# Local attention's q and k: projected by tokens and transposed, or projected by features

## The chip, the cores and the metric

The kernel runs on one core of a Trainium2 chip. The metric is device time in microseconds of one execution, as the median of several runs. Engines are named as in the profile: PE (TensorE, with PEld for its weight loads), DVE (VectorE), ACT (ScalarE), POOL (GpSimd) and SP (SyncE, whose queue issues all DMAs here).

## The reference

Eight sequences of 512 tokens with 128 features pass through a linear attention layer (16 heads, second-order Taylor features), a residual sum, and then six layers of local attention and a gated feed-forward network. The change is in the local attention, whose part of the reference is, for each layer:

```python
q, k, v = split(x @ Wqkv)                 # 16 heads of 64
q = l2norm(q) * qs;  k = l2norm(k) * ksc  # l2norm: t / max(|t|, 1e-12)
q = q * cos * scale + rotate_half(q) * sin * scale
k = k * cos * inv + rotate_half(k) * sin * inv      # inv = 1 / scale
# windows of 32 tokens; each sees itself and the window before
sim = einsum('bhwie,bhwje->bhwij', bq, bk2) * 8.0
attn = softmax(where(mask, -max, sim), -1)
out = einsum('bhwij,bhwje->bhwie', attn, bv2) @ Wo
# rotate_half([x1, x2]) = [-x2, x1], halves of 32
```

All of it is in float32.

## The kernel before

A first stage (some 500 us) computes the linear attention for all eight sequences. Then the six layers run over units: one unit is a block of 128 tokens of one sequence in one layer, 6 x 8 x 4 = 192 units in all. A loop over slots `t` starts one unit per slot; the steps of a unit are spread over several slots by `at(t, lag, step)`, which runs the step for unit `t - lag`. Each sequence's activations stay in SBUF, by features, in `state[b]` (128 features x 513 tokens). After the last of the four units of a sequence the feed-forward steps follow, in four successive slots: `feed_norm`, `feed_first` (transposes of the normalised tokens), `feed_middle` (three hidden chunks with Gelu, lines 667 to 675) and `feed_last` (w2, line 702).

PE's instructions run in the order in which the loop writes them (`manual_schedule`). The order on the other engines is made by the tile framework when it builds the program: it places instructions by their readiness in its own plan, puts those in `high_priority` ahead, and keeps what `issue_behind` asks for. Each engine then works through its list strictly in order.

Of PSUM's eight banks, four are two buffers of tag "mm" (projections, values, hidden chunks, w2), two are two buffers of tag "tr" (transposes), and two are the one buffer of tag "s". That last one is used in turn by `out_project` (py, line 642), `weigh_values` (po, line 613), and `masked` and `scores` (sp, lines 558 and 572). A step that takes a buffer waits until all readers of the one that had it before are done.

The steps of a unit before the change:

- `proj` (lag 0): q and k are projected with the tokens as the stationary operand, so that the result has tokens on partitions and 1024 columns (16 heads x 64) in PSUM. Line 451 is its matmul. DVE multiplies it by two tables out of PSUM (`turned`, line 459, and `straight`, line 467), ACT squares it (line 475, two halves), POOL sums the two products (line 482).
- `sum_squares`: DVE reduces the squares to one number for each token and head (line 485). `unit_length`: ACT takes the root of its inverse as Exp(-0.5 Ln) (lines 96 and 98), POOL bounds it (line 495) and multiplies q and k by it (line 498).
- `values`, `spread` (lag 0): v is projected (line 509), copied to SBUF by ACT (line 514) and spread over two windows' partitions by ten DMAs (lines 523 to 526).
- `by_features` (lag 1): 16 transposes by PE (line 70) and four copies by ACT (line 548) turn q and k to features on partitions: qT, kT. POOL copies the last 32 tokens of kT ahead for the next unit (line 551).
- `masked` (lag 1): ACT writes the mask into sp. `scores` (lag 1): 64 matmuls of 64x32 tiles add q k on top (line 572); DVE takes the maxima (line 580); ACT computes sixteen exps of 128x64 with the negated maximum as bias, one for each head (line 584); DVE sums the weights (line 590).
- `by_keys`, `weigh_values` (lag 2): transposes of the weights, copies pT by ACT (line 602), 64 matmuls with v (line 613), and the division by the sums on DVE (line 621).
- `out_by_features` (lag 2), `out_project` (lag 3): transposes, copies oT by ACT (line 635), eight matmuls with Wo (line 642) and the sum onto `state` by DVE (line 647).

Three `addr_align` calls pad PE's instruction stream at certain places.

The first stage has a root that goes through DRAM: `head_norm` sums squares by matmuls into 32 PSUM rows each (line 324), takes the root (lines 329 and 331), writes it to the DRAM tile `roots` (line 334) and reads it back spread over partitions (line 338); line 340 multiplies by it on DVE.

Of the kernel before, what the change touches and what calls it, by code (L numbers as in the profile page):

```python
# [15 lines left out]
P = 128  # L16
# [7 lines left out]
FILL = 16  # L24
IN_STEP = 98
# [3 lines left out]
def sandwich_kernel(ctx: ExitStack, tc: tile.TileContext, ins: dict, out: bass.AP):  # L29
# [23 lines left out]
    roots = [dram.tile([2, 2, 2, N], F32, tag=f"roots_{i}", name=f"roots_{i}") for i in range(2)]  # L53
    state = [const.tile([P, N + 1], F32, tag=f"state_{b}", name=f"state_{b}") for b in range(B)]
# [5 lines left out]
    vec = const.tile([P, NV + 1], F32, tag="vec", name="vec")  # L60
    g_c, b_c, b2_c = (vec[:, i * DEPTH : (i + 1) * DEPTH] for i in range(3))
    b1_c = vec[:, 3 * DEPTH : NV].rearrange("p (c l) -> p c l", l=DEPTH)
    gw = vec[:, NV : NV + 1]

# [8 lines left out]
    tables, exps, divisions, copies, pcopies, maxima = [], [], [], [], [], []  # L73
# [7 lines left out]
    def gelu_only():  # L81
        ld = nc.scalar.preload_act_table_set("gelu_and_others")
        issue_behind(ld, pcopies[-1])
        issue_behind(ld, exps[-1])
        tables.append(ld)
# [53 lines left out]
    HF = HD // 2  # L139
# [33 lines left out]
    for a in range(2):  # L173
        nc.vector.memset(of[HD * a : HD * (a + 1), a::2], 1.0)
    eps4 = const.tile([P, 1], F32, tag="eps4", name="eps4")
# [112 lines left out]
    def weigh(k):  # L288
# [14 lines left out]
        if s == len(STEPS) - 1:  # L303
# [3 lines left out]
                [P, 2, NB, P], F32, tag=("qT", "pT", "on", "oT", "sq", "sq")[i], name="yT"  # L307
# [92 lines left out]
    rot = const.tile([P, 4, NB, HD], F32, tag="rot", name="rot")  # L400
    nc.sync.dma_start(rot, ins["rotary"].rearrange("k (n p) d -> p k n d", p=P))
    qks = const.tile([P, 2, DEPTH, HD], F32, tag="qks", name="qks")
    for s, nm in enumerate(("q_scale", "k_scale")):
        nc.sync.dma_start(
            qks[:, s].rearrange("p l d -> p (l d)"),
            ins[f"L0_ffn_{nm}"].rearrange("l d -> (l d)").partition_broadcast(P),
        )

    def load_layer(l):
# [13 lines left out]
        tab = wl.tile([P, 4, NB, HD], F32, tag="tab", name=f"tab_{l}")  # L423
        for s in range(2):
            sc = qks[:, s, l, :]
            nc.gpsimd.tensor_tensor(
                tab[:, 2 * s], rot[:, 2 * s], sc.unsqueeze(1).to_broadcast([P, NB, HD]), ALU.mult
            )
            for a, o in ((0, HF), (HF, 0)):
                nc.gpsimd.tensor_tensor(  # L430
                    tab[:, 2 * s + 1, :, a : a + HF],
                    rot[:, 2 * s + 1, :, a : a + HF],
                    sc[:, o : o + HF].unsqueeze(1).to_broadcast([P, NB, HF]),
                    ALU.mult,
                )

        return dict(wqkv=wqkv, wo=wo, w1=w1, w2=w2, tab=tab)

    def proj(u, s):

        L, b, j = u["L"], u["b"], u["j"]
        wqkv, tab = L["wqkv"], L["tab"]
        lhs = state[b][:, j * P : (j + 1) * P]
        if s == 0:
            u["ss"] = f2.tile([P, 2, H], F32, tag="ss", name="ss")
            u["qk"] = f2.tile([P, 2, H, 2, HF], F32, tag="qk", name="qk")
        ss, qk = u["ss"], u["qk"]

        ps = psum.tile([P, 2, H, HF], F32, tag="mm", name="mm")
        for a in range(2):  # L450
            nc.tensor.matmul(  # L451
                ps[:, a].rearrange("p h d -> p (h d)"), lhs, wqkv[:, s, a, :], start=True, stop=True
            )
        sq = f2.tile([P, H, 2, HF], F32, tag="sq", name="sq")
        t1 = f2.tile([P, 2, H, HF], F32, tag="t1", name="t1")
        t2 = f2.tile([P, 2, H, HF], F32, tag="t2", name="t2")

        def turned():
            nc.vector.tensor_tensor(  # L459
                t2, ps[:, ::-1],  # L460
                tab[:, 2 * s + 1, j, :].rearrange("p (a d) -> p a d", a=2).unsqueeze(2)
                .to_broadcast([P, 2, H, HF]),
                ALU.mult,
            )

        def straight():
            nc.vector.tensor_tensor(  # L467
                t1, ps,
                tab[:, 2 * s, j, :].rearrange("p (a d) -> p a d", a=2).unsqueeze(2)
                .to_broadcast([P, 2, H, HF]),  # L470
                ALU.mult,
            )

        def squared(a):
            nc.scalar.activation(sq[:, :, a, :], ps[:, a], AF.Square)  # L475

        turned()
        straight()
        squared(0)
        squared(1)  # L480
        u["sq", s] = sq
        nc.gpsimd.tensor_tensor(qk[:, s].rearrange("p h a d -> p a h d"), t1, t2, ALU.add)  # L482

    def sum_squares(u, s):
        su = nc.vector.tensor_reduce(  # L485
            u["ss"][:, s], u["sq", s].rearrange("p h a d -> p h (a d)"), AX.X, ALU.add
        )
        if divisions:
            issue_behind(su, divisions[-1])

    def unit_length(u):

        ss, qk = u["ss"], u["qk"]
        inverse_root(ss, ss)
        nc.gpsimd.tensor_scalar(ss, ss, 1e12, None, ALU.min)  # L495
        for i in range(2):
            t = qk[:, i].rearrange("p h a d -> p h (a d)")
            nc.gpsimd.tensor_tensor(  # L498
                t, t, ss[:, i, :].unsqueeze(2).to_broadcast([P, H, HD]), ALU.mult
            )  # L500

# [10 lines left out]
    def spread(u):  # L512
        j, v0 = u["j"], u["v0"]
        cp = nc.scalar.copy(v0, u.pop("v0ps"))
        if copies:
            issue_behind(cp, copies[-1])
# [15 lines left out]
    def by_features(u, c, which=(0, 1)):  # L532

        j, qk, B_ = u["j"], u["qk"], u["B"]
        if c == 0:
            u["qT"] = f1.tile([P, NP, P], F32, tag="qT", name="qT")
            if j == 0:
                B_["kT"] = f2.tile([P, NP, W + P], F32, tag="kT", name="kT")
                nc.gpsimd.memset(B_["kT"][:, :, :W], 0.0)
            u["kT"] = B_["kT"]  # L540
        for s in which if isinstance(which, tuple) else (which,):
            ps = psum.tile([P, 4, P], F32, tag="tr", name="tr")
            for i in range(4):
                h0 = 2 * (c + i)
                transposed(ps[:, i, :], qk[:, s, h0 : h0 + 2].rearrange("p h a d -> p (h a d)"), P, P)
            dst = u["qT"][:, c : c + 4, :] if s == 0 else u["kT"][:, c : c + 4, W:]
            with tc.high_priority():
                copies.append(nc.scalar.copy(dst, ps))  # L548
        if c == NP - 4 and s == 1 and j < NB - 1:
            B_["kT"] = f2.tile([P, NP, W + P], F32, tag="kT", name="kT")  # L550
            nc.gpsimd.tensor_copy(B_["kT"][:, :, :W], u["kT"][:, :, P:])

    def masked(u):

        u["sp"] = sp = psum.tile([P, 2, NP, 2 * W], F32, tag="s", name="sp", bufs=1)
        mk = mask0 if u["j"] == 0 else mask
        with tc.high_priority():
            sd = nc.scalar.copy(
                sp.rearrange("t p c k -> t (p c) k"), mk.unsqueeze(1).to_broadcast([P, H, 2 * W])
            )  # L560
        issue_behind(sd, copies[-1])

    def scores(u):

        qT, kT = u["qT"], u["kT"]
# [13 lines left out]
        with tc.high_priority():  # L579
            maxima.append(nc.vector.tensor_reduce(mx, sp, AX.X, ALU.max, negate=True))  # L580
        pe = f2.tile([P, NP, 2, 2 * W], F32, tag="pe", name="pe")
        for pair in range(NP):
            for p in range(2):
                ex = nc.scalar.activation(  # L584
                    pe[:, pair, p, :], sp[:, p, pair, :], AF.Exp, bias=mx[:, p, pair : pair + 1]
                )
                issue_behind(ex, tables[-1])
        exps.append(ex)
        su = f2.tile([P, NP, 2], F32, tag="su", name="su")
        nc.vector.tensor_reduce(su, pe, AX.X, ALU.add)  # L590
        nc.vector.reciprocal(su, su)
        u["pe"], u["su"] = pe, su
# [69 lines left out]
    def feed_hidden(u, c):  # L662
# [5 lines left out]
        nc.tensor.addr_align(FILL, offset=FILL // 2)  # L668
        nc.tensor.matmul(pg[:cn, 1], w1[:, c0 : c0 + cn], xnT, start=True, stop=True)  # L669
        if c < NCH - 1:  # L670
            nc.tensor.addr_align(FILL, offset=FILL // 2)
# [85 lines left out]
    with tc.manual_schedule(engines={mybir.EngineType.PE}):  # L757
# [8 lines left out]
        for t in range(len(units) + 7):  # L766
# [7 lines left out]
            gelus = 0 <= t - 5 < len(units) and units[t - 5]["j"] == NB - 1  # L774
            at(t, 0, proj, 0)
            at(t, 0, proj, 1)


            if t % NB == 1 and NB < t < len(units):
                nc.tensor.addr_align(128, offset=IN_STEP)  # L780
            if t % NB == 3 and NB < t < len(units):
                nc.tensor.addr_align(FILL)
            at(t, 2, by_keys)
            if gelus:
                gelu_only()
            at(t, 3, out_project)
# [5 lines left out]
            at(t, 1, by_features, 0)  # L792
            at(t, 2, weigh_values)
            at(t, 1, by_features, 4, 0)
            at(t, 1, masked)
            at(t, 0, values)
            if t == 3:
                to_state(B - 1)
            at(t, 0, sum_squares, 0)
            at(t, 0, sum_squares, 1)  # L800
            if not gelus:
                at(t, 0, unit_length)
            at(t, 1, by_features, 4, 1)
            at(t, 0, spread)
            at(t, 3, feed_norm, ends=True)
            at(t, 4, feed_first, ends=True)

# [121 lines left out]
```

## Time and profile before

| what | value |
|---|---|
| median of 3 runs | 3645.83 us (3638.61 to 3646.25) |
| profiled execution, first to last instruction | 3641.2 us |
| granted PE clock, mean | 0.993 |
| PE matmuls busy | 3575.2 us (98%), 65184 instructions |
| PE weight loads busy | 2404.3 us (66%) |
| DVE busy | 2796.4 us (77%) |
| ACT busy | 2765.6 us (76%) |
| POOL busy | 1843.6 us (51%) |
| DMA queue, share of 16 engines | 25.2%, 240.93 MB |

Busy time counts an instruction from its start to its end, and matmuls overlap, so a PE that is 98% busy is not one at its peak. Idle time of an engine matters only where another waits for it. In the groups, a line counts two records for each float32 matmul and one for each transpose. The profile names each instruction by line, engine, operation and output <- input.

### The profile page before, as it was taken

Reading aid. Unit: us, or ns where it says so; the run is one execution under the profiler, and the core shown is the slowest. Engines: PE = TensorE matmul, PEld = TensorE weight load, DVE = VectorE, ACT = ScalarE, POOL = GpSimd, SP = SyncE. Lnnn points to the kernel's source line nnn. Section 1 sums busy time; section 2 is a strip of 40 time slices with the busy share of each in tenths; the row PEclk is TensorE's granted clock in tenths of the full one; section 3 lists DMA queues with packets and bytes.
Section 4 is the critical chain, followed back from the end, with each engine's and each line's share of the span. In section 5 each row is a group of like instructions: output and inputs, shape, how many; then the busy total and the mean of one; then the engine's idle time right before and its main releaser. Section 6 shows DMA issues by size and latency. Waiting matters only on the chain.

```text
span 3641.2 us, 153034 instructions
## 1 busy us (share of the span) xinstructions
PE 3575.2 (98%) x65184; PEld 2404.3 (66%) x65184; DVE 2796.4 (77%) x3915; ACT 2765.6 (76%) x6864; POOL 1843.6 (51%) x1311
## 2 busy tenths in 40 slices
PE   8999989999999999999999999999999999999997
PEld 4555556666766666676766766667676676766765
DVE  4555567887878788787887878878787887878885
ACT  4555557787888888888787888888878787887875
POOL 0000045555655556555565655556555565556652
PEclk9999999999999999999999999999999999999998
DMA  3121132222232222232222322223222222222221
GB/s 109 46 53 47 42 89 68 65 65 69 79 77 72 65 64 71 77 81 68 61 69 68 87 72 69 65 65 86 71 71 69 60 70 64 66 68 73 74 74 47
DMA packets 158598, 250.73 MB, mean 69 GB/s; under 512 B 33774, under 2 KB 54508, under 8 KB 157164
## 3 DMA queue, kind: packets, MB, share of 16 engines
q1 hardware_dynamic: 157932, 240.93, 25.2%
q8 instruction: 530, 8.68, 1.0%
q14 instruction: 136, 1.11, 0.1%
HBM read 41.31 MB, written 4.46 MB: 13 GB/s over the span
## 4 chain that ended last, share of the span: by engine, by line
PE 87%; ACT 9%; DVE 2%; issue 1%; DMA 1%; POOL 0%; SPq 0%; POOLq 0%; DVEq 0%; ACTq 0%
PE tr L70 19%; PE mm L451 14%; PE py L642 10%; PE mm L509 9%; PE po L613 8%; PE sp L572 6%; ACT pe L584 4%; PE mm L667 4%; PE mm L669 4%; PE y L299 3%; PE py L702 3%; PE sc L269 2%; PE po L348 2%; ACT L76 1%; PE vv L247 1%; ACT oT L635 1%
## 5 line engine op out<-in xcount | busy, mean ns | idle before, releaser
L482 POOL TENSOR_TENSOR qk<-t,t 128x1024 f32<-128x1024 f32 x384 | 910.9, 2372 | 619.1 <-DVE t L467 424.7
L498 POOL TENSOR_TENSOR qk<-qk,ss 128x1024 f32<-128x1024 f32 x384 | 722.4, 1902 | 16.0
L451 PE MATMUL mm<-wqkv,state 128*128 128x512 f32 x1536 | 700.3, 596 | 0.6 <-issue 0.6
L584 ACT ACTIVATE pe<-sp,mx 128x64 f32<-128x64 f32 x3072 | 652.0, 381 | 2.4 <-DVE mx L580 2.3
L459 DVE TENSOR_TENSOR t<-mm,tab 128x1024 f32<-128x1024 f32 x384 | 468.3, 1219 | 220.3 <-PE mm L451 214.9
L475 ACT ACTIVATE sq<-mm 128x512 f32<-128x512 f32 x768 | 420.6, 605 | 127.4 <-DVE t L467 120.9
L467 DVE TENSOR_TENSOR t<-mm,tab 128x1024 f32<-128x1024 f32 x384 | 468.1, 1219 | 5.9
L451 PEld LDWEIGHTS mm<-wqkv,state 128*128 128x128 f32 x1536 | 273.1, 190 | 289.8 <-issue 242.4
L485 DVE TENSOR_REDUCE ss<-sq 128x16 f32<-128x1024 f32 x384 | 448.4, 1209 | 0.1
L70 PE MATMUL tr<-ident,qk 128*128 128x128 f32 x3072 | 440.9, 276 | 1.8 <-ACT qT L548 0.8
L70 PEld LDWEIGHTS tr<-ident,qk 128*128 128x128 f32 x3072 | 351.3, 141 | 120.7 <-issue 56.3
L642 PE MATMUL py<-oT,wo 128*128 128x128 f32 x3072 | 379.3, 277 | 0.3 <-ACT oT L635 0.3
L642 PEld LDWEIGHTS py<-oT,wo 128*128 128x128 f32 x3072 | 368.1, 196 | 0.5 <-ACT oT L635 0.5
L509 PE MATMUL mm<-wqkv,state 128*128 128x512 f32 x768 | 362.9, 595 | 2.6 <-DVE t L467 2.6
L635 ACT COPY oT<-tr 128x512 f32<-128x512 f32 x384 | 205.5, 587 | 168.1 <-PE tr L70 165.5
L572 PEld LDWEIGHTS sp<-kT,qT 64*32 64x32 f32 x24576 | 264.2, 105 | 91.3 <-issue 54.3
L613 PE MATMUL po<-v,pT 64*32 64x64 f32 x24576 | 297.0, 225 | 9.6 <-issue 3.9
L548 ACT COPY qT<-tr 128x512 f32<-128x512 f32 x384 | 226.3, 589 | 99.6 <-PE tr L70 99.1
L613 PEld LDWEIGHTS po<-v,pT 64*32 64x32 f32 x24576 | 268.8, 105 | 46.0 <-PE tr L70 24.6
L572 PE MATMUL sp<-kT,qT 64*32 64x64 f32 x24576 | 297.6, 225 | 0.3 <-issue 0.3
L495 POOL TENSOR_SCALAR ss<-ss 128x32 f32<-128x32 f32 x192 | 54.7, 285 | 478.7 <-ACT ss L98 470.8
L548 ACT COPY kT<-tr 128x512 f32<-128x512 f32 x384 | 225.6, 588 | 74.8 <-PE tr L70 74.5
(110 smaller groups left out, 5243.9 us busy)
## 6 DMA issues: line engine op xcount, KB each, us to landing
v<-v SPq DMA_DIRECT2D x1152, 128.0 KB
v<-v SPq DMA_DIRECT2D x672, 64.0 KB
rs<-roots SPq DMA_DIRECT2D x64, 256.0 KB
wqkv<-in_L_ffn_Wqkv_dram SPq DMA_DIRECT2D x6, 1536.0 KB
wo<-in_L_ffn_Wo_dram SPq DMA_DIRECT2D x6, 512.0 KB
xin<-_attn_hidden_states_dram SPq DMA_DIRECT2D x8, 256.0 KB
xr<-_attn_hidden_states_dram SPq DMA_DIRECT2D x8, 256.0 KB
x<-xr SPq DMA_DIRECT2D x8, 256.0 KB
```

What stands on the lines that cost most here:

```text
L70: nc.tensor.transpose(ps[:cols, :rows], src, ident[:rows, :rows])
L451: nc.tensor.matmul(ps[:, a].rearrange("p h d -> p (h d)"), lhs, wqkv[:, s, a, :], start=True, stop=True)
L459: nc.vector.tensor_tensor(t2, ps[:, ::-1], tab[:, 2 * s + 1, j, :].rearrange("p (a d) -> p a d", a=2).unsqueeze(2) .to_broadcast([P, 2, H, ...
L467: nc.vector.tensor_tensor(t1, ps, tab[:, 2 * s, j, :].rearrange("p (a d) -> p a d", a=2).unsqueeze(2) .to_broadcast([P, 2, H, HF]), ALU.mult,)
L482: nc.gpsimd.tensor_tensor(qk[:, s].rearrange("p h a d -> p a h d"), t1, t2, ALU.add)
L498: nc.gpsimd.tensor_tensor(t, t, ss[:, i, :].unsqueeze(2).to_broadcast([P, H, HD]), ALU.mult)
L509: nc.tensor.matmul(ps[:, p, :], lhs, L["wqkv"][:, 2, p, :], start=True, stop=True)
L548: copies.append(nc.scalar.copy(dst, ps))
L572: nc.tensor.matmul(sp[W * w : W * (w + 1), p, pair, :], qT[HD * p : HD * (p + 1), pair, W * w : W * (w + 1)], kT[HD * p : HD * (p + 1), pa ...
L584: ex = nc.scalar.activation(pe[:, pair, p, :], sp[:, p, pair, :], AF.Exp, bias=mx[:, p, pair : pair + 1])
L613: nc.tensor.matmul(po[W * w : W * (w + 1), p, pair, :], pT[r, pair, W * w : W * (w + 1)], v2[r, w, HD * pair : HD * (pair + 1)], start=(pa ...
L642: nc.tensor.matmul(py, L["wo"][:, c, :], oT[:, c, :], start=(c == 0), stop=(c == NP - 1))
```

## The change

q and k are now projected with the weights as the stationary operand, 128 features (two heads) at a time, so that they come out with features on partitions, and the transposes and copies of `by_features` go. The halves of a head are no longer beside each other on one partition, so the order of features in the weights and tables is permuted in such a way that rotating by half is a swap of 16 with 16 partitions inside each group of 32: a DVE `stream_shuffle`. POOL takes over the product with the second table.

The squares' sums now run over partitions: 16 matmuls with a matrix of ones (`per_head`), each into 32 PSUM rows. The roots of k are written to a DRAM tile `lengths` and read back spread over 64 partitions each, and POOL multiplies k by them into kT. The roots of q are not multiplied into q: they are transposed by PE (`lengths_by_tokens`) to one number for each token and head, and are given to the exps as their scale; the negated maxima are multiplied by them first, on DVE.

The steps behind the scores have moved by one slot (`by_keys`, `weigh_values` lag 3, `out_project` lag 4, feed-forward steps each one later), `values` and `spread` run one slot later too, and the sum of the weights is a step of its own a slot after the exps. The tables are loaded from DRAM for each layer and scaled on POOL. The pads in PE's stream and several `issue_behind` go.

```diff
     def proj(u, s):
-        ps = psum.tile([P, 2, H, HF], F32, tag="mm", name="mm")
-        for a in range(2):
-            nc.tensor.matmul(
-                ps[:, a].rearrange("p h d -> p (h d)"), lhs, wqkv[:, s, a, :], start=True, stop=True
-            )
...
-        turned()
-        straight()
-        squared(0)
-        squared(1)
-        nc.gpsimd.tensor_tensor(qk[:, s].rearrange("p h a d -> p a h d"), t1, t2, ALU.add)
+        ps = psum.tile([P, NP, P], F32, tag="mm", name="mm")
+        for c in range(NP):
+            nc.tensor.matmul(
+                ps[:, c], L["wqkv"][:, s].rearrange("p a c -> p (a c)")[:, c * P : (c + 1) * P],
+                state[b][:, tok], start=True, stop=True,
+            )
...
+        with tc.high_priority():
+            nc.scalar.activation(sq, ps, AF.Square)
+        nc.vector.stream_shuffle(t2.rearrange("p c n -> p (c n)"), ps.rearrange("p c n -> p (c n)"), swap)
+        nc.vector.tensor_tensor(t1, ps, tab[0], ALU.mult)
+        nc.gpsimd.tensor_tensor(t2, t2, tab[1], ALU.mult)
+        nc.gpsimd.tensor_tensor(u["qk"][:, s], t1, t2, ALU.add)
...
-    def sum_squares(u, s):
-        su = nc.vector.tensor_reduce(
-            u["ss"][:, s], u["sq", s].rearrange("p h a d -> p h (a d)"), AX.X, ALU.add
-        )
+    def sum_squares(u):
+        u["ms"] = ms = psum.tile([P, 2, P], F32, tag="tr", name="ms")
+        for s in range(2):
+            sq = u.pop(("sq", s))
+            for r in range(2):
+                for i in range(4):
+                    nc.tensor.matmul(
+                        ms[W * i : W * (i + 1), s], per_head[:, r], sq[:, 2 * i + r],
+                        start=(r == 0), stop=(r == 1), skip_group_check=True,
+                    )
...
     def unit_length(u):
-        inverse_root(ss, ss)
-        nc.gpsimd.tensor_scalar(ss, ss, 1e12, None, ALU.min)
-        for i in range(2):
-            t = qk[:, i].rearrange("p h a d -> p h (a d)")
-            nc.gpsimd.tensor_tensor(
-                t, t, ss[:, i, :].unsqueeze(2).to_broadcast([P, H, HD]), ALU.mult
-            )
+        rt = f2.tile([P, 2, P], F32, tag="rt", name="rt")
+        with tc.high_priority():
+            inverse_root(rt, u.pop("ms"))
+        nc.gpsimd.tensor_scalar(rt, rt, 1e12, None, ALU.min)
+        rd = lengths[u["j"] % 2]
+        for a in range(2):
+            nc.sync.dma_start(rd[a], rt[8 * a : P : 16, 1])
+        rs = f1.tile([P, NP, P], F32, tag="rs", name="rs")
+        for a in range(2):
+            nc.sync.dma_start(
+                rs[HD * a : HD * (a + 1)].rearrange("p c n -> p (c n)"),
+                rd[a].rearrange("c n -> (c n)").partition_broadcast(HD),
+            )
...
+        nc.gpsimd.tensor_tensor(u["kT"][:, :, W:], u["qk"][:, 1], rs, ALU.mult)
+        if u["j"] < NB - 1:
+            B_["kT"] = f2.tile([P, NP, W + P], F32, tag="kT", name="kT")
+            nc.gpsimd.tensor_copy(B_["kT"][:, :, :W], u["kT"][:, :, P:])
+
+    def lengths_by_tokens(u):
+        ps = psum.tile([P, H, 8], F32, tag="tr", name="qr")
+        transposed(ps.rearrange("p h k -> p (h k)"), u.pop("rt")[:, 0], P, P)
+        u["qr"] = qr = f2.tile([P, NP, 2], F32, tag="qr", name="qr")
+        nc.vector.tensor_copy(qr.rearrange("p c a -> p (c a)"), ps[:, :, 0])
...
-    def by_features(u, c, which=(0, 1)):
...
     def scores(u):
...
             maxima.append(nc.vector.tensor_reduce(mx, sp, AX.X, ALU.max, negate=True))
+            nc.vector.tensor_tensor(mx, mx, qr.rearrange("p c a -> p a c"), ALU.mult)
...
                 ex = nc.scalar.activation(
-                    pe[:, pair, p, :], sp[:, p, pair, :], AF.Exp, bias=mx[:, p, pair : pair + 1]
+                    pe[:, pair, p, :], sp[:, p, pair, :], AF.Exp,
+                    bias=mx[:, p, pair : pair + 1], scale=qr[:, pair, p : p + 1],
                 )
...
             at(t, 0, proj, 0)
             at(t, 0, proj, 1)
-            at(t, 2, by_keys)
+            at(t, 3, by_keys)
+            at(t, 0, sum_squares)
+            at(t, 0, unit_length)
...
-            at(t, 3, out_project)
+            at(t, 4, out_project)
...
-            at(t, 1, by_features, 0)
-            at(t, 2, weigh_values)
-            at(t, 1, by_features, 4, 0)
+            at(t, 3, weigh_values)
+            at(t, 2, weight_sums)
             at(t, 1, masked)
-            at(t, 0, values)
+            at(t, 1, values)
...
+            at(t, 0, lengths_by_tokens)
+            at(t, 7, feed_last, ends=True)
             at(t, 1, scores)
```

## The prediction

> **What bounds the kernel now.** The page's head first, then the chain that ended last, then the timeline of one steady slot, instruction by instruction.
>
> ```profile
> PE 3575.2 (98%) x65184; PEld 2404.3 (66%) x65184; DVE 2796.4 (77%) x3915; ACT 2765.6 (76%) x6864; POOL 1843.6 (51%) x1311
> ...
> PE 87%; ACT 9%; DVE 2%; issue 1%; DMA 1%; POOL 0%; SPq 0%; POOLq 0%; DVEq 0%; ACTq 0%
> ```
>
> By this page TensorE (PE) sets the pace. The timeline of the slot at 2000 us shows what stands close behind it:
>
> ```profile
> 2004.14 1.95 PE L642 MATMUL py<-oT,wo 128*128 128x128 f32 x16
> ...
> 2006.32 0.58 DVE L647 TENSOR_TENSOR state<-py,state 64x128 f32<-64x128 f32 x2
> ...
> 2007.01 1.48 PE L613 MATMUL po<-v,pT 64*32 64x64 f32 x128
> ...
> 2008.52 1.23 DVE L621 TENSOR_TENSOR on<-po,su 128x1024 f32<-128x1024 f32 x1
> ...
> 2009.91 1.05 ACT L558 CAST sp<-mask 128x1024 f32<-128x1024 bf16 x1
> ...
> 2011.59 1.48 PE L572 MATMUL sp<-kT,qT 64*32 64x64 f32 x128
> ...
> 2013.18 1.23 DVE L580 TENSOR_REDUCE mx<-sp 128x16 f32<-128x1024 f32 x1
> ...
> 2013.93 3.79 PE L451 MATMUL mm<-wqkv,state 128*128 128x512 f32 x8
> ...
> 2014.66 3.40 ACT L584 ACTIVATE pe<-sp,mx 128x64 f32<-128x64 f32 x16
> ```
>
> py, po and sp share PSUM's one buffer "s", so these rows are a ring: py, state sum, po, division, mask, scores, maxima, sixteen exps, and only then the next py. The exps end at 2018.06; the next py starts at 2018.44, and in the slot before 2003.92 is followed by 2004.14. The ring is therefore already full: 14.13 us, from projection start 1999.80 to 2013.93, is both PE's sum and the ring's. Projection starts in this stretch are 1899.42, 1918.75, 1935.47, 1949.60 and 1963.84: four slots (hidden chunks, w2, two ordinary) are 64.4 us, times 48 is 3091 us of the span of 3641.2.
>
> **PE alone.** From the chain's own starts, the sixteen q/k transposes are 0.89 + 0.59 + 0.44 = 1.92 us a slot, and they go. The projections become 16 matmuls of py's form (1.79 us for 8): 3.58 instead of 3.44. The sums of squares are 16 matmuls into 32 columns. The nearest row is head_norm's (L324, 512 wide, 17.0 us for 64 = 0.266, against 0.911 for a full 128x512 at L451), so quarters overlap and 128 wide costs 0.066 each, 1.06 together; without overlap it is 3.58. I take 1.06, same form. The one transpose of the roots is 0.11. PE's net: 0.14 - 1.92 + 1.06 + 0.11 = -0.61 a slot, -117 us in 192. Other engines lose work too: four copies by ScalarE (0.59 each), two VectorE reductions (1.21 each), and the squares are one instruction in place of two. The shuffle takes the place of a product out of PSUM of the same size (1.22).
>
> **The ring after.** In the built program's order ScalarE no longer runs its sixteen exps together. A slot reads: mask, v0, two oT, 5 exps, Square q, 3 exps, Square k, two pT, 3 exps, Ln, 1 exp, Exp, 4 exps. py still waits for the last exp. Where the roots and squares stood in the ring's shadow, they stand in it now. From the scores' start (0):
>
> - Maxima 1.59 to 2.82 (2011.59 to 2013.18, then 1.23). The new product of maxima and q roots, 0.25 (a 128x16 reciprocal is 0.253), to 3.05. Exps from 3.15, oT being done by then.
> - An exp follows an exp after 0.20 (3.39 = 15 x 0.20 + 0.38). The exps get a second operand by row, the scale. What one costs: copies run 0.589 at 512 and 1.02 at 1024, 0.84 ns an element; two copies of 512 follow each other after 0.485, thus 0.054 + 0.054 = 0.108 for 64 elements without such an operand, and 0.20 with one. A second then adds 0.09; the bounds are 0 (fetched beside the first) and 0.09. I take 0.29, since the small Ln rows say the same (ln_rs with eps 0.296, its Exp without 0.205).
> - 5 exps to 4.6. Square q 1.03 to 5.63 (its projection ends at 2.34 + 1.80 = 4.14). 3 exps 6.50, Square k 7.53, two pT 1.07 to 8.60, 3 exps 9.47. The sums wait for the first pT, which frees their PSUM buffer (8.1), and end at 9.2, just hidden; unoverlapped they would add 2.3. Ln and Exp of 128x256 by the same slope 0.40 and 0.38; with 5 exps and a tail of 0.18 the last ends at 11.88.
> - py 0.2 later. py to po 2.87, po to division 1.51, division to mask 1.39, mask 1.05, 0.15 to the scores: 6.97, all from the rows above. Scores again at 19.07.
>
> An ordinary slot is thus 19.1 us against 14.13. With exps at 0.20 the Squares and Ln wait 0.5 in all for PE, and it is 18.1. The feed-forward slots: values end 6.0 after py starts; three hidden chunks take 5.54 (1910.82 to 1916.36), so scores come 4.6 later than in an ordinary slot; w2 2.6 and the root transpose, 1.75 later; the layer norm's first row stands between maxima and product, 0.3. Four slots: 4 x 19.07 + 6.65 = 82.9.
>
> **GpSimd and the new product.** GpSimd's queue in a slot is t2 q, add q, t2 k, minimum, add k, kT product, copy of k's last tokens. A full 128x1024 product or sum is 2.37 (L482; the products by table go by 2.13 ns an element from the rows of 128 and 256, also 2.37): 5 x 2.37 + 0.45 + 0.40 = 12.7 against 9.1 (two sums, two products at 1.90, minimum, copy). The kT product waits for the roots' way through DRAM, queued on it is the next slot's t2. The same round trip is in the first stage:
>
> ```profile
> 485.18 1.12 SPq L334 DMA_DIRECT2D roots<-rt  x4
> 487.58 3.39 SPq L338 DMA_DIRECT2D rs<-roots  x4
> ...
> 492.25 2.79 DVE L340 SCALAR_TENSOR_TENSOR yT<-yT,vec,rs 128x1024 f32<-128x1024 f32 x1 [3.70 <-DMA rs<-roots]
> ...
> 490.20 3.76 POOL L498 TENSOR_TENSOR qk<-qk,ss 128x1024 f32<-128x1024 f32 x2
> ```
>
> From root to consumer 6.65 and 7.1 us, with four writes; here there are two, so 6.5. The shuffle of q waits for Square q (5.63), t2 q starts at 7.1, the minimum ends at 14.65, kT runs 21.15 to 23.5. PE does not need kT before the scores at 38, so its way is hidden, with 14 us to spare, and SyncE's four more issues stand ahead of v's ten, which wait for the mask anyway. But the last two rows show a collision: L340, whose inputs both lie in SBUF, takes 1.27 elsewhere and 2.79 while GpSimd works, ending 1.1 after it. The product of maxima and roots reads two SBUF tiles. After a slot of 19.07 it is due at 19.07 + 2.82 = 21.9, inside kT's run, and would finish at 23.6: 1.7 lost. After a hidden-chunk or w2 slot kT is done (23.7, 20.8 long). So two of four slots lose 1.7: 86.3. Bounds: 0 (it slips ahead of kT) and 2.37.
>
> Four slots go from 64.4 to 86.3, +21.9; times 48 is +1051. One more slot of drain (+10; 0 to 20); table loads and start 0, lost alignment pads of PE's queue 0, as PE has slack then. 3641.2 + 1061 = 4702; the median of the runs lies 4.6 over the span: 4707.
>
> **The clock.** Where PE waited for exps in the drain, it lost half its clock:
>
> ```profile
> 3577.00:3580.60 3.60, 2.40 (x8) 1.08 (x9) 0.12 (x1) 3.43 (x15) 2.15 (x2) 1.00 0.65 166
> 3580.60:3582.00 1.40, 1.40 (x8) 1.40 (x9) 1.35 (x2) 1.09 (x2) 0.00 (x0) 0.52 0.62 181
> 3582.00:3584.30 2.30, 2.30 (x14) 2.30 (x14) 0.02 (x1) 0.78 (x1) 0.00 (x0) 0.55 0.00 0
> ```
>
> (The third figure from the end of each row is the granted clock; the pairs before it are the busy time of PE, its weight loads, VectorE, ScalarE and GpSimd.) py took 3.58 there instead of 1.95. In the new slot PE does 1.06 us of work between 6.8 and 12.1, a thinner stretch than 3577 to 3580.6, right ahead of py. If each py pays 1.7, that wait takes the place of the lost 1.7 at kT, and only the other two slots grow: 89.7, 4870. The Trainium skill ("TensorE: Matmul & The Clock Gate", section "Why this matters for your kernels") warns only of idle gaps beyond about 3 us. The gap ahead of py is 2.9 by this reckoning, so by that rule the clock stays and the sum is 4707; the rows above have no gap that long and the clock fell. I leave it out of the number and in the range, since the drain also had a thin stretch at nearly full clock (3610 to 3620 us, PE busy 6.4 of 10, clock 0.91).
>
> **Rivals.**
> 1. Forecast: ring with the second operand's price and the product's wait: 4707. Chance 0.40.
> 2. Cheaper ring: operand free, product ahead of kT: 4 x 18.1 + 6.65 = 79.05, +703 + 15: 4360; one of both, about 4500. For it: both prices rest on few rows. Chance 0.27.
> 3. The clock falls in each slot: 4870. Chance 0.25.
> 4. Faster: PE stays the bound. Place: py. If the exps ended when PE arrives there (sums done, about 8.0 after the scores), the slot would be PE's 13.5 and the time 3646 - 117 = 3529. It decides at 8.0 against my 11.9; for that the Squares, roots and pT (4.0 us) would have to stand behind the exps. PE's 98% speaks for it, the built order against it. Chance 0.05.
> 5. More than one of the above at its worst (sums unoverlapped): over 4910. Chance 0.03.
>
> **How the numbers follow.** Cases 1 to 3 span 4360 to 4870; with the drain and kT's bounds 4340 to 4910, which leaves out case 4, case 5 and some of the low edge. Slower by over 0.2% (about what a measurement of this kernel can tell from no change) is 0.95, faster 0.04 and same 0.01, the last for a case 4 eaten up by the drain.
>
> **What would show it.** PE's share near 75% and ScalarE, with GpSimd, in the chain; py waiting 2 us or more for the exps in nearly every slot; exps 0.29 apart; the small product by q roots over 1 us in half of its runs; mean clock near 0.99 (case 1) or clearly below (case 3); slots of 19 to 21 us. Wrong it is if py waits for nothing, or if slots stay under 16.

## The result and the profile after

The changed kernel takes 4932.5 us (median of 4 runs, 4909.7 to 4945.3), the kernel before 3644.6 beside it (3638.6 to 3646.3): 1.353 times as long, 95% interval 1.349 to 1.357. The prediction was 4707, with a range from 4340 to 4910, which misses the time by 22 us.

The page's head of the profiled execution (span 4907.8 us), and its row of the granted clock in tenths, 40 slices:

```profile
PE 3955.2 (81%) x73056; PEld 3026.5 (62%) x73056; DVE 2486.9 (51%) x4304; ACT 2666.1 (54%) x5712; POOL 2586.0 (53%) x1491
...
PEclk9999788888988888889888888988898989888888
```

No engine is busy all the time, which fits a ring. PE's clock is 8 in most slices; in before it is 9 in all but the last:

```profile
PEclk9999999999999999999999999999999999999998
```

One slot of after, instruction by instruction, in the form in which the prediction showed the slot of before:

```profile
2707.19 1.59 PE L544 MATMUL sp<-kT,qk 64*32 64x64 f32 x128
...
2708.89 1.23 DVE L552 TENSOR_REDUCE mx<-sp 128x16 f32<-128x1024 f32 x1
...
2710.36 1.61 ACT L557 ACTIVATE pe<-sp,mx,qr 128x64 f32<-128x64 f32 x5
...
2717.29 1.32 ACT L557 ACTIVATE pe<-sp,mx,qr 128x64 f32<-128x64 f32 x4
2718.66 3.78 PE L623 MATMUL py<-oT,wo 128*128 128x128 f32 x16 [2.37 <-ACT pe L557]
...
2723.18 1.89 PE L594 MATMUL po<-v,pT 64*32 64x64 f32 x128 [0.73 <-PE py L623]
...
2725.15 1.22 DVE L602 TENSOR_TENSOR on<-po,su 128x1024 f32<-128x1024 f32 x1 [2.07 <-PE po L594]
2726.46 1.02 ACT L531 CAST sp<-mask 128x1024 f32<-128x1024 bf16 x1 [7.85 <-DVE on L602]
2727.53 1.48 PE L544 MATMUL sp<-kT,qk 64*32 64x64 f32 x128
```

The ring is the one described: scores, maxima, exps, py, po, division, mask, scores. Measured from the scores, the first exps start at 3.17 us (3.15 predicted), the last exp ends at 11.42 (11.88) and py starts at 11.47 (12.1). From there on it is longer than predicted: py to po takes 4.52 us against 2.87, po to division 1.97 against 1.51. The slot shown is one of those with the most loss there: averaged over 186 slots of the trace, the scores start 12.07 us ahead of py, py 4.03 us ahead of po and po 2.07 us ahead of the division (12.1, 2.87 and 1.51 predicted). On average, too, the surplus lies behind py. The windows of the same stretch say why (pairs of busy time for PE, weight loads, VectorE, ScalarE, GpSimd, then granted clock, DMA share, GB/s):

```profile
2716.40:2718.60 2.20, 0.00 (x0) 0.00 (x0) 1.39 (x2) 2.20 (x8) 2.12 (x2) 0.79 0.00 0
2718.60:2720.50 1.90, 1.84 (x8) 1.84 (x9) 0.00 (x0) 0.01 (x1) 1.90 (x2) 0.50 0.00 0
2720.50:2722.40 1.90, 1.90 (x10) 1.65 (x8) 0.00 (x0) 0.00 (x0) 1.90 (x3) 0.50 0.00 0
2722.40:2725.00 2.60, 1.87 (x130) 1.76 (x129) 0.58 (x2) 0.00 (x0) 2.27 (x1) 0.59 0.05 9
```

While PE waits for the exps its clock starts to fall; py and most of po then run at half of it. The waits view agrees on where PE stands (us in total, times, longest). Its rows here are, in this order: ScalarE's mask, at the ring's other end, waiting for the division; GpSimd's product of k and the roots, waiting for DRAM; py, waiting for the exps; and the exps, waiting for the small product by q roots:

```profile
ACT sp L531 <- DVE on L602: 1355.4, 190, 10.3
...
POOL kT L486 <- DMA rs<-lengths: 776.6, 184, 6.6
...
PE py L623 <- ACT pe L557: 458.8, 190, 5.4
...
ACT pe L557 <- DVE mx L553: 63.5, 66, 5.9
```

### The profile page after: what moved, and what is told of

Same layout as the page of the kernel before. It is cut to its first block, busy times and chain, and to the rows that moved or that the text cites. A ratio compares the mean times of both kernels' runs of the same rounds, so it can differ in the third digit from the quotient of the medians.

```text
span 4907.8 us, 165148 instructions
## 1 busy us (share of the span) xinstructions
PE 3955.2 (81%) x73056; PEld 3026.5 (62%) x73056; DVE 2486.9 (51%) x4304; ACT 2666.1 (54%) x5712; POOL 2586.0 (53%) x1491
## 5 line engine op out<-in xcount | busy, mean ns | idle before, releaser
L449 POOL TENSOR_TENSOR t<-t,tab 128x1024 f32<-128x1024 f32 x384 | 908.3, 2365 | 754.4 <-DVE t L447 748.0
L557 ACT ACTIVATE pe<-sp,mx,qr 128x64 f32<-128x64 f32 x3072 | 1046.7, 442 | 65.8 <-DVE mx L553 63.5
L486 POOL TENSOR_TENSOR kT<-qk,rs 128x1024 f32<-128x1024 f32 x192 | 453.4, 2361 | 791.1 <-DMA rs<-lengths 776.6
L437 PE MATMUL mm<-state,wqkv 128*128 128x128 f32 x6144 | 740.4, 278 | 29.0 <-DVE xn L113 20.1
L437 PEld LDWEIGHTS mm<-state,wqkv 128*128 128x128 f32 x6144 | 716.0, 194 | 37.8 <-DVE xn L113 27.0
L447 DVE STREAM_SHUFFLE t<-mm 128x1024 f32<-128x1024 f32 x384 | 507.8, 1322 | 2.4 <-issue 0.7
L505 PE MATMUL mm<-wqkv,state 128*128 128x512 f32 x768 | 467.7, 739 | 7.0 <-issue 6.9
L448 DVE TENSOR_TENSOR t<-mm,tab 128x1024 f32<-128x1024 f32 x384 | 464.1, 1209 | 0.2 <-PE ms L330 0.2
L446 ACT ACTIVATE sq<-mm 128x1024 f32<-128x1024 f32 x384 | 406.4, 1058 | 20.8 <-PE mm L437 20.7
L544 PE MATMUL sp<-kT,qk 64*32 64x64 f32 x24576 | 305.3, 226 | 21.0 <-issue 12.8
```

What stands on the lines that cost most here:

```text
L437: nc.tensor.matmul(ps[:, c], L["wqkv"][:, s].rearrange("p a c -> p (a c)")[:, c * P : (c + 1) * P], state[b][:, tok], start=True, stop=True,)
L446: nc.scalar.activation(sq, ps, AF.Square)
L447: nc.vector.stream_shuffle(t2.rearrange("p c n -> p (c n)"), ps.rearrange("p c n -> p (c n)"), swap)
L448: nc.vector.tensor_tensor(t1, ps, tab[0], ALU.mult)
L449: nc.gpsimd.tensor_tensor(t2, t2, tab[1], ALU.mult)
L486: nc.gpsimd.tensor_tensor(u["kT"][:, :, W:], u["qk"][:, 1], rs, ALU.mult)
```

## The experiments

"before" and "after" are the two kernels; every run is a kernel made from one of them by the edit shown. Ratios are against before, measured beside the run, with their 95% intervals. fill4, prodps, nodram, sqlate and pyktps rest on two runs each, the others on four or five.

### The clock: filling PE's wait

```diff
 # loop over slots, PE's order
             at(t, 0, sum_squares)
             at(t, 0, unit_length)
+            if 4 <= t < len(units):
+                fill(16)       # 16 transposes of ident into a "tr" buffer
             ...
             at(t, 4, out_project)
```

> 16 more transposes of 128x128 (about 1.9 us at full clock) stand on PE between the sums and py, in the stretch in which PE waits for the last exps. Nothing else differs. If the granted clock sets part of the slot (it reads 0.50 to 0.59 from py to the division after that wait), py to po falls from 4.52 to about 2.9 and po to division from 1.97 to 1.5, 2.1 us a slot; then the loop of GpSimd's products and the small product by q roots (21.4 us) takes over in part, and I expect about 4750 (4650 to 4850). If the clock does not matter, PE has only more work ahead of py: 4930 or more.

4614.8 us, ratio 1.265 (1.263 to 1.267): 318 us less than after, with more work on PE. The timeline of the run:

```profile
2707.51 1.97 PE L70 MATMUL fill<-ident 128*128 128x128 f32 x16
...
2709.94 2.05 PE L629 MATMUL py<-oT,wo 128*128 128x128 f32 x16 [0.46 <-ACT pe L563]
...
2712.73 1.58 PE L600 MATMUL po<-v,pT 64*32 64x64 f32 x128 [0.73 <-PE py L629]
...
2714.35 1.23 DVE L608 TENSOR_TENSOR on<-po,su 128x1024 f32<-128x1024 f32 x1 [1.73 <-PE po L600]
```

py waits for the exps still, but starts 0.46 us after PE's last work instead of 2.37. py to po is 2.79 and po to division 1.62, the prediction's 2.87 and 1.51. Averaged over the slots, py to po is 2.78 us where after has 4.03, and po to division 1.84 where it has 2.07; scores to py is not shorter (12.38 against 12.07). So the gain lies behind py, where the clock had been low. It is larger than expected (4650 at best): GpSimd's loop did not take over, for GpSimd still waits 578 us in all for VectorE's shuffles. A smaller filling shows how much of it is needed:

```diff
-                fill(16)
+                fill(4)
```

> after with 4 instead of 16 transposes of filling on PE between the sums and py, 0.5 us of the wait of about 2.4. If the clock falls only after a wait of more than about 2 us, this nearly keeps it: 4620 to 4720. If what counts is the share of work in the whole stretch, half of the loss or more remains: 4750 to 4930.

4699.1 us, ratio 1.290 (1.287 to 1.293): 0.5 us of work recovers three quarters of what 1.9 us does. The time lies in the range of the first case. In the slot shown the wait is 1.77 and py runs at full clock:

```profile
2718.56 2.05 PE L629 MATMUL py<-oT,wo 128*128 128x128 f32 x16 [1.77 <-ACT pe L563]
```

But not in every slot. py's 16 rows, with the idle time ahead of them, read from the timeline over the steady part (540 to 4860 us) of four runs:

| run | median wait ahead of py | py over 2.4 us (full clock: 1.95 to 2.05) |
|---|---|---|
| after | 2.37 | 168 of 187 |
| noprod (below) | 2.36 | 157 of 189 |
| fill4 | 1.77 | 66 of 191 |
| fill | 0.46 | 2 of 188, those behind waits of over 5 us |

So the length of the wait does not decide alone. The clock records in the traces show what goes with the fall. They know two clocks, full and half, and the changes lie on a fixed grid: in the steady part of after, the distances between the starts of the falls are whole multiples of 3.4133 us. Cut into the windows of that grid, the steady parts of the fourteen traces (from 540 us to 70 us before the end) have 13987 windows at full clock. Of those in which PE was busy for less than 40% of the time, all 850 were followed by a window at half clock; between 40 and 50%, 301 of 611; above 50%, 4 of 12526. In these traces the share of work in such a window thus tells the fall better than the wait does, and the same wait lies differently on the grid from slot to slot. (The drain of before is less clear: two windows that read 66 and 67% busy were followed by half clock too.)

### The second operand of the exps

```diff
 # the kernel before
-  pe[...], sp[...], AF.Exp, bias=mx[:, p, pair : pair + 1]
+  pe[...], sp[...], AF.Exp, bias=mx[:, p, pair : pair + 1],
+  scale=unit[:, 0:1],          # a column of ones
```

The pT copies were kept behind the exps by `issue_behind`; ScalarE's order moves by a Square or two.

> The kernel before, with a scale operand by row (a column of ones) on its 16 exps; nothing is computed otherwise. If a second operand costs 0.09 on each exp (0.20 to 0.29 apart, as in after), and PE's ring through the scores' buffer has no slack, 16 x 0.09 = 1.4 us a slot, +270: about 3920. If PE has slack there (its 98% comes from its own work): 3650 to 3700. If the operand is free: 3645.

3902.9 us, ratio 1.071 (1.070 to 1.073), +260 of the 278 that 192 x 16 x 0.09 gives.

```profile
2713.79 4.85 ACT L587 ACTIVATE pe<-sp,mx,unit 128x64 f32<-128x64 f32 x16
```

The sixteen exps take 4.85 us where before took 3.40: 0.09 each. Nearly all of it reaches the end, with no work added to PE. So the ring of before had next to no slack, though PE read 98% busy and looked like the only bound. Whether PE's own sum had any was not tried.

### py out of the ring

```diff
-        py = psum.tile([P, P], F32, tag="s", name="py", bufs=1)
+        py = psum.tile([P, P], F32, tag="tr", name="py")
```

> py goes to the PSUM tag of the transposes instead of the one-buffer tag of scores and po, so it no longer waits for the last exp; po still does. If the ring on that buffer sets the slot, py (about 2.9 to 4.5 us with its half clock) leaves the ring and the slot falls from 22.7 to 18.2 to 21.4: 4050 to 4700, the lower end if GpSimd's own five products (about 17.8 with the wait for the roots from DRAM) bind next, the upper one if the product by q roots still waits behind them. If the ring is not the bound: 4930.

4124.1 us, ratio 1.131 (1.129 to 1.134): one line takes back 808 of the 1288 us. py no longer waits for the exps, so PE has work in that gap and its mean clock is 0.974 instead of 0.882. What waits now:

```profile
POOL kT L486 <- DMA rs<-lengths: 745.6, 169, 8.2
...
PE po L594 <- ACT pe L557: 78.1, 177, 3.2
```

PE hardly waits for exps any more (78 us against 459), while GpSimd's wait for DRAM is nearly what it was (746 us against 777) and each engine has the same work to do. This shows the ring through the buffer "s", not PE, GpSimd or DRAM, as what set the slots of after. The 808 us hold the clock's share too, which fill puts at about 318. What sets the slots of this run was not tried by itself.

### The small product and GpSimd

```diff
-            nc.vector.tensor_tensor(mx, mx, qr.rearrange("p c a -> p a c"), ALU.mult)
...
+        nc.vector.tensor_scalar(su, su, 1e-30, None, ALU.add)
```

> The product of maxima and q roots is left out (the exps' bias is then the maximum of the unscaled scores, so the weights are not the reference's), and the weight sums get 1e-30 added by an instruction of 0.3 us off the ring. The trace of after has this product at 468 ns mean against 176 undisturbed, 192 times: 90 us in all, 56 of them lost to GpSimd's products. If it lies in the ring: about 4840 (4800 to 4860). If the ring is set by something else that merely ends last with it: 4930. If its wait also holds GpSimd back and so the loop of both: below 4800.

4867.5 us, ratio 1.336 (1.333 to 1.339): 65 us less, not 90, and 7 us above the expected range. ScalarE's two oT copies end about when the undisturbed product does (2710.48 and 2710.33 us in the slot shown above), which fits that mostly the collisions are saved. Two rows of after show one, with the exps behind it, and a row of its groups has all 192 of these products (busy us, mean ns, idle before):

```profile
2729.80 2.36 POOL L486 TENSOR_TENSOR kT<-qk,rs 128x1024 f32<-128x1024 f32 x1 [5.13 <-DMA rs<-lengths]
...
2730.58 1.61 DVE L553 TENSOR_TENSOR mx<-mx,qr 128x16 f32<-128x16 f32 x1
...
2732.23 1.29 ACT L557 ACTIVATE pe<-sp,mx,qr 128x64 f32<-128x64 f32 x4 [1.52 <-DVE mx L553]
```

```profile
L553 DVE TENSOR_TENSOR mx<-mx,qr 128x16 f32<-128x16 f32 x192 | 89.8, 468 | 4.8
```

The product of 128x16 ends with GpSimd's. The next run asks what the collision is over:

```diff
+        u["qrps"] = ps.rearrange("p (c a) k -> p a c k", a=2)[:, :, :, 0]   # the transpose's own tile
...
-            nc.vector.tensor_tensor(mx, mx, qr.rearrange("p c a -> p a c"), ALU.mult)
+            nc.vector.tensor_tensor(mx, mx, u.pop("qrps"), ALU.mult)
```

> after, with one edit: the small product of maxima and q roots reads the roots from the PSUM tile that the transpose leaves, so only one of its inputs lies in SBUF. If GpSimd blocks a VectorE operation only where both inputs are in SBUF, its mean falls from 468 ns to about 176 and the time by up to 56 us: 4875 to 4930. If GpSimd blocks it as it did: the mean stays at 450 or more, and the time at 4930, or above it because the second copy of oT's transposes then waits for that PSUM buffer.

5010.6 us, ratio 1.375 (1.372 to 1.379), slower than after. Its rows have the short product of the first case and the wait for the buffer of the second:

```profile
2715.97 2.34 POOL L486 TENSOR_TENSOR kT<-qk,rs 128x1024 f32<-128x1024 f32 x1 [5.61 <-PE sp L545]
...
2717.12 0.17 DVE L554 TENSOR_TENSOR mx<-mx,qr 128x16 f32<-128x16 f32 x1
...
2717.35 0.65 PE L70 MATMUL tr<-ident,on 128*128 128x128 f32 x4 [1.71 <-DVE mx L554]
```

```profile
L554 DVE TENSOR_TENSOR mx<-mx,qr 128x16 f32<-128x16 f32 x192 | 32.1, 167 | 4.8
```

In the middle of GpSimd's product the small one now takes 0.17 us (mean of all 192: 167 ns instead of 468). 38 of the 192 start while a product or sum of GpSimd runs, and none takes over 0.18 us. But oT's transposes wait for its PSUM buffer (319 us in all), and with them what stands behind. The Trainium skill ("SBUF — State Buffer", section "SBUF: two separate sides") says that a VectorE operation with two SBUF inputs is locked out while a GpSimd operation reads SBUF, and the other way round. These rows agree with the first half; none of them shows the other.

### The way through DRAM

```diff
-        nc.gpsimd.tensor_tensor(u["kT"][:, :, W:], u["qk"][:, 1], rs, ALU.mult)
+        nc.gpsimd.tensor_tensor(u["kT"][:, :, W:], u["qk"][:, 1], ones, ALU.mult)
```

> The product of k and the roots reads a constant tile of ones instead of the roots brought back from DRAM, so k stays unscaled and the output is not the reference's; the transfers are still issued, nobody waits for them. In after GpSimd waits 776.6 us in all (184 times, up to 6.6) for them. If that wait costs only through the small product by q roots, which then starts before GpSimd's product and not beside it, I expect 4850 to 4890 (the collision's 56 us gone). If the way through DRAM itself sets the slot: 4.0 us less in each, about 4150.

4876.6 us, ratio 1.339 (1.336 to 1.341): 56 us less, give or take some 20 by the two intervals, which is about the collision's 56 (the small product's mean falls to 181 ns). GpSimd's product does not come a whole wait earlier, for now it waits for the scores, which read kT:

```profile
POOL kT L491 <- PE sp L546: 653.0, 140, 9.1
```

So the 777 us that GpSimd waits for the roots from DRAM cost nothing else that this run shows, as long as the ring is the bound.

### The Squares behind the exps

```diff
-        with tc.high_priority():
-            nc.scalar.activation(sq, ps, AF.Square)
         ...                                       # the shuffle
         nc.vector.tensor_tensor(t1, ps, tab[0], ALU.mult)
+        s2 = nc.scalar.activation(sq, ps, AF.Square)
+        if weights:
+            issue_behind(s2, weights[-1])         # the last of the 16 exps
 # loop: sum_squares and unit_length move from ahead of out_project to behind weigh_values
```

> The two Squares go behind the 16 exps on ScalarE, the sums behind po on PE, the shuffles ahead of the Squares on VectorE; what is computed is the same. The last exp then ends about 9.0 us after the scores begin (3.15 + 16 x 0.29 + two copies of pT 1.07) against 11.4 in after, so py 2.4 us earlier: about 4470 if PE's clock still falls in the wait ahead of py (its gap is then longer, without the sums), about 4200 if the clock stays. If the Squares and roots between the exps cost nothing: 4930. The roots' way ends later; if GpSimd's queue behind it sets the slot: above 4600.

4875.1 us, ratio 1.338 (1.335 to 1.341), which only the last case, above 4600, allows for. py does come earlier (in the slot at 2717 us 9.85 after the scores), but the gain is taken back elsewhere:

```profile
2726.72 2.05 PE L624 MATMUL py<-oT,wo 128*128 128x128 f32 x16 [2.00 <-ACT pe L558]
...
2735.31 0.85 POOL L471 TENSOR_SCALAR rt<-rt 128x256 f32<-128x256 f32 x1
2736.22 0.33 PE L70 MATMUL qr<-ident,rt 128*128 128x128 f32 x1 [1.77 <-POOL rt L471]
```

The roots come later, their minimum stands behind k's sum on GpSimd, and the transpose of q roots, which PE has to do ahead of the scores, waits for it (174 us in all, 134 times). ScalarE has 138 more instructions, table loads of 1.28 us for Ln, for Exp and for gelu itself (46 each), and the clock still falls in the wait ahead of py (105 of 187 slots). How the 57 us net divide among these was not tried.

### Putting them together

```diff
 # shortened; all four: py in "tr"; transpose of q roots one slot later (lag 1); product
 # reads PSUM; k's product is a step of its own (keys_scaled), one slot later
-            at(t, 0, lengths_by_tokens)
+            at(t, 1, lengths_by_tokens)
 # pyktps: keys_scaled behind the next unit's second product and sum on GpSimd
+            at(t, 0, proj, 0); at(t, 0, proj, 1); at(t, 1, keys_scaled)
 # best:   the same, and the Squares behind the exps
 # best2:  keys_scaled between the two, the minimum behind the second product by table
+            at(t, 0, proj, 0); at(t, 1, keys_scaled); at(t, 0, proj, 1)
 # best3:  and gelu's table loaded behind the roots
-            if gelus: gelu_only()      # ahead of out_project
+            if gelus: gelu_only()      # behind unit_length
```

> py in the transposes' tag as in the run before, and two things more: the product of k and roots goes behind the next unit's four products and sums on GpSimd's queue, so that nothing is queued behind its wait for DRAM, and the product of maxima and q roots reads the roots from PSUM, one operand less in SBUF. The ring is then scores to last exp 11.4, po 1.5, division 1.4, mask 1.05 and small gaps, 15.7 an ordinary slot: about 3850 (3750 to 3950). If GpSimd's waits did not set the slot of the run before: 4120 as there. If the collision was not for SBUF: about 56 us over the ring's number.

4615.8 us, ratio 1.267 (1.265 to 1.270), 492 us slower than with py moved alone. By the waits view the larger part is that the scores now wait for k:

```profile
PE sp L554 <- POOL kT L494: 419.3, 139, 8.6
```

The PSUM buffer that the small product holds may add a share: oT's second transposes wait 130 us in all for the copy of the first, where one buffer is left. Its price was not measured.

> All of it: py in the transposes' tag, Squares, sums and roots behind the exps, k's product behind the next unit's products, the small product from PSUM; the result is the reference's. The ring is about 13 us a slot, PE's own work 13.5, GpSimd's five products, minimum and copy 13.1: three nearly equal bounds. If PE alone binds: about 3530 to 3650. If they disturb each other (a wait of one is not made up by the next): 3700 to 3900. If PE's clock falls in its wait for the pT copies: above 3900.

4515.1 us, ratio 1.239 (1.237 to 1.242), with the same wait:

```profile
PE sp L555 <- POOL kT L495: 343.0, 138, 4.1
```

Both expectations counted the ring and each engine's load, and neither counted the new loop that a queue makes: scores, projection, shuffle, four GpSimd operations, k's product, scores. In one slot of pyktps these start at 2711.10 (scores), 2714.52 (projection) and 2719.14 us (the first of the four), k's product runs from 2728.66 to 2731.00, and the next scores start at 2731.06.

> As the run before with everything put together, but k's product stands between the two units of GpSimd's queue that the next q and k need: next q's product and sum, then k's product, then next k's. In the run before it stood behind all four and the scores waited for it (343 us on PE, 138 times), with a slot of 20 us. By the rows of that run the scores then find kT about 13.1 us after the scores before, and PE's own work sets the slot at 14.1 to 14.7: 3650 to 3800. If the wait only moves (to the minimum, to the q roots or to the DRAM way): 3800 to 4300. If the order on GpSimd's queue was not the cause: 4515.

4143.4 us, ratio 1.137 (1.135 to 1.139), in the second case's range. PE's wait for k is all but gone (22 us), which shows the order on GpSimd's queue as its cause; an ordinary slot is 15.4 us (scores at 2646.53 and 2661.91). Longer are the slots with gelu, where ScalarE changes its table for the roots (rows of that run):

```profile
2674.69 1.28 ACT L97 ACT_TABLE_LOAD   x1 [0.21 <-issue]
...
2677.30 1.28 ACT L99 ACT_TABLE_LOAD   x1
```

> As the run before, with one thing moved: ScalarE's table for gelu is loaded behind the roots' Ln and Exp instead of ahead of them, so the roots of that slot need no loads of their own (two of 1.28 us in one slot of four). Ordinary slots stay at 15.4 us, where PE hardly waits. If the loads were on the path: 4143 less 48 x 2.6 to 48 x 5, about 3900 to 4020. If they were hidden: 4143.

4059.7 us, ratio 1.114 (1.112 to 1.117), 84 us less, short of the range. Three loads of 1.28 us go in nearly every such slot, the roots' two and gelu's own second one (46 each). The gain is 1.75 us in each of 48 slots, less than their 3.85, so part of them was hidden. It is the fastest form of the changed kernel here, and 11% slower than before. What it still waits for on PE is spread out (the waits view of best3):

```profile
PE tr L70 <- ACT oT L628: 130.1, 192, 1.0
...
PE ms L465 <- issue: 77.6, 48, 3.4
...
PE py L635 <- ACT pT L595: 63.3, 189, 1.2
```

No version beat the kernel before.

## Why the prediction was right or wrong

**Direction and mechanism: right.** Slower, with the ring through "s" as the bound. pytr shows it by taking py out, nodram by finding the DRAM way hidden, b_scale by finding the ring of before full.

**The exps and their second operand: right.** 0.09 each was predicted from copies and small Ln rows; b_scale measured 0.09, and after's exps follow each other 0.29 to 0.30 apart. The bound of 0, which carried rival 2 (4360 to 4500, chance 0.27), had no support in a run. In the slot shown every offset up to py came out within 0.65 us; on average py starts 12.07 us behind the scores, where 12.1 was reckoned.

**The clock: this step failed.** The prediction saw half clock in the drain, reckoned what it would cost in each slot, and then wrote "I leave it out of the number and in the range". The clock did fall: in 168 of 187 slots, and filling PE's wait gave 318 us back. Case 3 had the right mechanism with too low a chance (0.25) and too low a price (4870). It let the lost clock take the place of the lost 1.7 us at k's product, as if only one of the two could be paid, and so charged two slots of four. Both are paid: with the clock restored (fill) the collision is 69 us, with the clock low 56. It also counted py alone, where po runs slow as well (1.65 + 0.46 us in the slot shown, 1.25 + 0.23 on average against fill). Its 1.7 in all 192 slots would have been 326 us, near the measured 318. The top of the range, 4910, rested on this case and fell short with it.

The evidence weighed against the clock's fall was one thin stretch of the drain, 3610 to 3620 us, at clock 0.91. The rows at 3580 us, with py itself in them, were the nearer ones. PE reads about as busy in both stretches (64 and 67%), so the drain could not decide. The new slot was far thinner: the prediction itself had 1.06 us of work in 5.3 there, so that a window of 3.41 us inside it has 31% at most, under the 40% behind which the clock fell every time in the steady part. The page of the Trainium skill that the prediction named ("TensorE: Matmul & The Clock Gate", section "Why this matters for your kernels") warns of idle gaps beyond about 3 us. By that rule the clock would have stayed; in after it fell behind waits of 2.37 us, and in a third of fill4's slots behind 1.77. Here the measurement decides.

**The collision: mechanism right, size wrong.** "Two of four slots lose 1.7" is 3.4 per four slots, 163 us. Measured are 468 - 176 = 292 ns a slot, 56 us, and nodram and noprod gave back 56 and 65. The sign that the prediction named, over 1 us in half of the runs, shows in 31 of 192. Two of the four kinds of slots is right: 55 of the 59 products over 0.3 us stand in them. But they are little more than half of these 96 slots, and most lose less than 1.7. That the phase between the two queues shifts from slot to slot, where the sum took it as fixed, is likely and was not tried.

**The sum mended.** 4707 - 107 (collision) + 318 (clock) = 4918, against 4932.5 measured. With fill, where the clock stays and the small product has a mean of 536 ns (69 us of collision), the forecast would be 4707 - 94 = 4613; measured 4614.8. This is one check and not two, since the 318 is the difference of the two runs. By it the slot was reckoned rightly but for these two terms, the clock left out and the collision too large. They had opposite signs, so that the time came out within 5% of the forecast is partly luck.

**Small errors without effect.** GpSimd's minimum of 128x256 takes 0.85 us where 0.45 was taken, hidden beside the ring in after (PE waits 9.8 us in all for it); in sqlate, where PE waits 174 us, such an error counts. The root's transpose takes 0.27 us where 0.11 was taken. The 0 for the lost pads in PE's stream was not tried.

**The rival on the other side.** Case 4 (3529) asked for the Squares and roots behind the exps and a PE sum that is 117 us smaller. best3 does the first. By its rows the replaced work is smaller as reckoned: the sums of squares (232.8 us), the transposes of roots (52.6) and the projections (741.4) stand against projections (700.3) and q and k transposes (440.9) in before, 114 us less where 117 was forecast. Yet PE's busy time as a whole is 3629.0 us against 3575.2, since other rows are longer there: v's projection 408.3 against 362.9, the transposes for oT 258.4 against 209.7. So the saving never reached the time. Why those rows are longer was not tried.

## What to carry to other kernels

When a buffer with one copy is handed through several engines, add up that ring as well as each engine: an engine at 98% may hide a ring that is just as full, and what is moved onto it is paid nearly in full, 260 of 278 us here. When a forecast makes TensorE wait in every slot, add up its work in stretches of 3.4 us around the wait (in the steady parts here the clock fell behind every window under 40%), price the work behind the wait at half clock, and add that price to the others instead of letting one replace the other. When an operation is moved on a queue, draw the new loop from its result back to what it waits for: k's product, moved out of one wait, made PE wait 419 us at the scores.

## What was not expected of the hardware

PE's granted clock fell to 0.50 behind waits of only 2.37 us, and no length of the wait divides the slots: behind 1.77 us py ran slow in 66 of 191 slots, behind waits near 0.46 in none. What divides them better is PE's share of work in the windows of a fixed grid of 3.4133 us: under 40% the next window was at half clock 850 times of 850, above 50% 4 times of 12526. Sixteen useless transposes in such a wait saved 6% of the kernel's time, four of them 5%. And a 128x16 product that read one input from PSUM was not held up by GpSimd in any of its 192 runs (167 ns mean, 172 at most), where the same product from SBUF took up to 2.36 us.
